# One word instead of 512 cleared between two scatters of a routed transformer kernel, with the order of work laid out anew

## The chip, the core and the metric

The kernel runs on one core of one Trainium2 chip. The time is device microseconds of one execution; where several runs are shown, the median is given with its lowest and highest. The core's engines are named as the profile names them: PE multiplies matrices (PEld is its weight load), DVE and ACT work on vectors, POOL (GpSimd) does small vector work and issues the scatters, SP (SyncE) issues the plain transfers. Each engine runs its own instructions strictly in the order in which the program emitted them; between engines semaphores hold an instruction until what it reads is there.

## What is computed

Two layers over `x` of 4 batches x 512 tokens x 128 features, each layer a cross-attention (16 heads of 8, against a context of 77 positions) and then a mixture of 8 experts of which each token uses 2:

```python
x = x + tanh(g_xattn[0]) * L0_xattn(layernorm(x), ctx_1024, Wq, Wk, Wv, Wo, bo)
x = x + tanh(g_ffn[0])   * L0_ffn(layernorm(x), w_router, w1, b1, w2, b2)
x = x + tanh(g_xattn[1]) * L1_xattn(layernorm(x), ctx_1024, ..., positions, mask)
x = x + tanh(g_ffn[1])   * L1_ffn(layernorm(x), gate_w, w1, b1, w2, b2)
```

In L0_ffn and L1_ffn a softmax over 8 router logits gives two experts and their weights; each expert is 128 -> 512 -> GELU -> 128 with biases, and the two results are added with their weights. In the second layer's attention a position bias and a mask are added to the scores, and the softmax has 1 added to its denominator.

## The kernel before

All arithmetic is in f32. A batch of 512 tokens is held as 128 partitions x 4 tokens. The four batches form two groups of two, and each group of 1024 tokens is routed by itself, in each layer: every token is written twice (once for each of its two experts) to a DRAM table `xg` in which each expert has a region of rows. The tokens are then read back in blocks of rows that belong to one expert, 7 blocks of 256 rows and 9 of 128 for each group, multiplied with that expert's weights, and the result rows are written to a second DRAM table `yk`, at rows that belong to the tokens. Last the two result rows of each token are loaded and added to `x`.

Both writes are scatters: POOL issues an indirect DMA that writes 128 rows, one from each partition, to the rows named by 128 indices. There are 64 into `xg` (4 batches x 4 x 2 for each of two layers) and 92 into `yk` (one for each 128 rows of a block). `Scatters.send` issues them all. Ahead of each it clears 512 words on one partition of `fill`, the tile of zeros that was written to the `xg` tables at the start. No scatter reads that tile.

What is emitted when is written out by hand in the text `ORDER`; an engine meets its instructions in that order. A word is a layer, a part, a number, and a batch or group after the dot:

- Attention of a batch: `LS` statistics, `LT` shift and norm, `LU` transposition, `Q` queries, `S0` to `S3` scores and their maxima (DVE, line 297), `M` minus the maximum, `W0`, `W1` that put into the queries, `X0` to `X3` scores once more and exponentials (ACT, line 335), `U0` to `U3` product with the values (PE, line 343), `E`, `T`, `N` division, `F` output projection and residual.
- Routing of a batch: `RS`, `RT`, `RU` the norm again, `RL` logits, `RC`, `RD` the two experts, `RM`, `RN` places by counting, `RX` the row numbers, `Z0` to `Z3` the scatters into `xg`, two in each.
- For a group: `RB` the table of blocks, `RG` its transposition and the read of the blocks' first rows into registers of SP (line 572). Everything that SP issues after this read in the order waits behind it.
- A block of a group: `w` load of the expert's weights (line 599, five buffers), `x` load of its rows (line 607, six buffers), `t` transposition, `u` first product and GELU (lines 634 and 640), `d` second product, bias and weight (lines 649 to 668), `y` its one or two scatters into `yk` (eight buffers).
- `CL`, `CA`: load of a batch's result rows and addition to `x`.
- At the start: `fill` clears the tile of zeros (DVE), `clear00` to `clear11` write it to the four `xg` tables (SP, lines 744 and 750), `vclear` clears a tile for values (POOL), `second` prepares constants of the second layer (POOL, from the loads of positions), `mask`, `routing`, `gate` prepare theirs.

The scatters of one target are declared independent of each other, so one does not wait for another's data; each eighth one waits for the scatter eight earlier, whose semaphore it uses again.

Of the kernel before, what the change touches and what calls it, by code (L numbers as in the profile page):

```python
# [8 lines left out]
F32 = mybir.dt.float32  # L9
# [7 lines left out]
B, S, D = 4, 512, 128  # L17
# [25 lines left out]
def flamingo_kernel(ctx: ExitStack, tc: tile.TileContext, a: dict, out: bass.AP):  # L43
    nc = tc.nc
# [3 lines left out]
    const = ctx.enter_context(tc.tile_pool(name="const", bufs=1))  # L48
# [51 lines left out]

    ident = const.tile([P, P], F32, tag="ident", name="ident")
    make_identity(nc, ident)
    mhalf = const.tile([P, NT], F32, tag="mhalf", name="mhalf")
    nc.gpsimd.memset(mhalf, -0.5)

# [280 lines left out]
    class Scatters:  # L386
# [4 lines left out]

        def send(self, to, rows, index):

            nc.gpsimd.memset(fill[:1, 0, :S], 0.0)  # L394
            i = nc.gpsimd.indirect_dma_start(  # L395
                out=to[:, :], out_offset=bass.IndirectOffsetOnAxis(ap=index, axis=0), in_=rows, in_offset=None
            )
            for other in self.sent:
                tc.declare_no_dep(i.ins, other.ins, reason="each pair has a row of its own")
            self.sent.append(i)  # L400
# [334 lines left out]
    fill = const.tile([P, 2, CAP // P * PAY], F32, tag="fill", name="fill")  # L735
# [75 lines left out]
    def part(l, name, n):  # L811
# [18 lines left out]
            }[name]()  # L830

    ORDER = """
        vclear3 vclear0 fill vclear2 0LS.0 keys0 gate values0 0LT.0 0LS.2 0LU.0 0LS.1 0LS.3 0Q.0 0LT.1 0LT.2 values3
        0S1.0 0S0.0 0S2.0 0LU.1 0LU.2 0S3.0 0Q.1 clear10 0M.0 vclear1 mask0 0W0.0 0LT.3 0S0.1 0W1.0 0S3.1 clear00
        0X0.0 0S1.1 0Q.2 values1 mask1 0S2.2 mask2 0X1.0 0S2.1 0U0.0 0M.1 0X2.0 routing 0U1.0 0X3.0 0E0.0 0W0.1 0U2.0
        0X0.1 0T0.0 0U3.0 0X1.1 0W1.1 0U0.1 0E1.0 0S1.2 0U1.1 0T1.0 clear01 mask3 0S0.2 0E0.1 0LU.3 clear11 0N.0 0T0.1
        0X2.1 0F.0 0RS.0 0X3.1 values2 0U2.1 0RT.0 0S3.2 0U3.1 0M.2 0E1.1 second 0Q.3 0W0.2 0RU.0 0T1.1 0W1.2 0S2.3
        0N.1 0RL.0 0RC.0 0F.1 0RS.1 0X0.2 0X1.2 0RD.0 0U0.2 0X2.2 0RM.0 0RN.0 0RX.0 0U1.2 0Z0.0 0RT.1 0S1.3 0U2.2
        0RU.1 0Z1.0 0S3.3 0RL.1 0S0.3 0X3.2 0RC.1 0M.3 0RD.1 0Z2.0 0U3.2 0W0.3 0RM.1 0E0.2 0T0.2 0X0.3 0RN.1 0RX.1
        0RB.1 0E1.2 0Z3.0 0X1.3 0Z0.1 0T1.2 0N.2 0RG.1 0U0.3 0W1.3 0w0.0 0Z1.1 0F.2 0Z2.1 0Z3.1 0x0.0 0U1.3 0RS.2  # L840
        0E0.3 0X2.3 0x1.0 0X3.3 0RT.2 0w1.0 0U2.3 0U3.3 0E1.3 0T0.3 0RU.2 0T1.3 0RL.2 0N.3 0RC.2 0t0.0 0x2.0 0t1.0
        0F.3 0RD.2 0x3.0 0w2.0 0x4.0 0u0.0 0u1.0 0RS.3 0RM.2 0d0.0 0x5.0 0w3.0 0w4.0 0w5.0 0y0.0 0RT.3 0d1.0 0t2.0
        0t3.0 0RN.2 0x6.0 0u2.0 0RU.3 0RX.2 0t4.0 0w6.0 0u3.0 0x7.0 0Z0.2 0d2.0 0u4.0 0t5.0 0RL.3 0t6.0 0d3.0 0x8.0
        0RC.3 0u5.0 0Z1.2 0RD.3 0RM.3 0d4.0 0u6.0 0RN.3 0y1.0 0d5.0 0d6.0 0RX.3 0w7.0 0w8.0 0Z2.2 0t7.0 0u7.0 0RB.3
        0w9.0 0x9.0 0y2.0 0d7.0 0w10.0 0Z3.2 0t8.0 0Z0.3 0RG.3 0t9.0 0w0.1 0x10.0 0w11.0 0u8.0 0Z1.3 0d8.0 0x11.0
        0Z2.3 0u9.0 0Z3.3 0t10.0 0w12.0 0d9.0 0x12.0 0u10.0 0y3.0 0x13.0 0d10.0 0w13.0 0x0.1 0t11.0 0t12.0 keys1 0x1.1
        0u11.0 0w1.1 0u12.0 0d11.0 0t0.1 0y4.0 0w14.0 0t1.1 0y5.0 0d12.0 0x2.1 0x14.0 0u0.1 0t13.0 0w2.1 0u1.1 0d0.1
        0y6.0 0x15.0 0y7.0 0u13.0 0y8.0 0y9.0 0y10.0 0x3.1 0t14.0 0t2.1 0w15.0 0d1.1 0u2.1 0w3.1 0t3.1 0y11.0 0d13.0
        0u14.0 0t15.0 0d2.1 0w4.1 0u15.0 0x4.1 0x5.1 0w5.1 0d14.0 0x6.1 0y12.0 0w6.1 0y13.0 0y14.0 0x7.1 0d15.0 0u3.1
        0t4.1 0t5.1 0x8.1 0w7.1 0d3.1 0u4.1 0t6.1 0u5.1 0y15.0 0d4.1 0t7.1 0u6.1 0x9.1 0CL.0 0t8.1 0w8.1 0y0.1 0y1.1  # L850
        0CA.0 1LS.0 0CL.1 0d5.1 0u7.1 0x10.1 0w9.1 0CA.1 1LT.0 0x11.1 0d6.1 0t9.1 0u8.1 0t10.1 0d7.1 1LU.0 1LS.1 0u9.1
        0d8.1 0y2.1 0y3.1 1Q.0 0t11.1 0w10.1 1LT.1 0x12.1 1S0.0 0w11.1 0d9.1 0y4.1 0y5.1 1S1.0 0x13.1 1LU.1 0u10.1
        0t12.1 0w12.1 1S2.0 0y6.1 0x14.1 0d10.1 0u11.1 0x15.1 1Q.1 0t13.1 0y7.1 1S3.0 0u12.1 0d11.1 0t14.1 0w13.1
        1S2.1 0y8.1 0w14.1 1S0.1 0d12.1 1M.0 0y9.1 0u13.1 0w15.1 1S3.1 1W1.0 0y10.1 0u14.1 0d13.1 1W0.0 0y11.1 0t15.1
        1S1.1 0y12.1 0u15.1 1X0.0 0d14.1 0d15.1 0y13.1 0y14.1 1X1.0 0y15.1 1U0.0 1M.1 1X2.0 1U1.0 0CL.2 1W0.1 1E0.0
        0CL.3 1X3.0 0CA.2 1U2.0 1X0.1 1LS.2 1U3.0 1E1.0 1T0.0 1X1.1 1W1.1 1LT.2 1T1.0 1U0.1 1N.0 1X2.1 1U1.1 1LU.2
        1F.0 0CA.3 1RS.0 1E0.1 1X3.1 1T0.1 1Q.2 1LS.3 1RT.0 1S1.2 1S3.2 1RU.0 1S2.2 1LT.3 1U2.1 1S0.2 1M.2 1U3.1 1E1.1
        1RL.0 1T1.1 1W0.2 1LU.3 1RC.0 1RD.0 1N.1 1X0.2 1F.1 1X1.2 1RS.1 1Q.3 1RM.0 1RN.0 1RX.0 1Z0.0 1W1.2 1RT.1 1S0.3
        1S1.3 1U0.2 1RU.1 1Z1.0 1S2.3 1RL.1 1X2.2 1U1.2 1Z2.0 1RC.1 1RD.1 1RM.1 1X3.2 1Z3.0 1RN.1 1RX.1 1S3.3 1Z0.1
        1M.3 1U2.2 1U3.2 1E0.2 1T0.2 1Z1.1 1E1.2 1Z2.1 1W0.3 1T1.2 1X0.3 1W1.3 1RB.1 1Z3.1 1N.2 1X1.3 1F.2 1U0.3 1RG.1  # L860
        1x0.0 1RS.2 1X2.3 1RT.2 1w0.0 1U1.3 1E0.3 1RU.2 1X3.3 1RL.2 1t0.0 1U2.3 1w1.0 1x1.0 1RC.2 1U3.3 1E1.3 1u0.0
        1RD.2 1RM.2 1RN.2 1x2.0 1RX.2 1x3.0 1x4.0 1T0.3 1T1.3 1N.3 1Z0.2 1F.3 1x5.0 1Z1.2 1t1.0 1w2.0 1RS.3 1d0.0
        1u1.0 1y0.0 1RT.3 1d1.0 1RU.3 1t2.0 1t3.0 1RL.3 1RC.3 1w3.0 1w4.0 1u2.0 1u3.0 1RD.3 1RM.3 1t4.0 1Z2.2 1RN.3
        1RX.3 1RB.3 1d2.0 1x6.0 1t5.0 1Z3.2 1Z0.3 1u4.0 1d3.0 1w5.0 1w6.0 1w7.0 1w8.0 1RG.3 1t6.0 1u5.0 1Z1.3 1x7.0
        1d4.0 1x8.0 1u6.0 1t7.0 1x9.0 1w9.0 1Z2.3 1Z3.3 1d5.0 1x10.0 1d6.0 1u7.0 1d7.0 1y1.0 1t8.0 1x11.0 1x0.1 1y2.0
        1w0.1 1u8.0 1y3.0 1t9.0 1y4.0 1u9.0 1t10.0 1t0.1 1x1.1 1d8.0 1w10.0 1u0.1 1d9.0 1t1.1 1u10.0 1t11.0 1y5.0
        1y6.0 1x2.1 1w11.0 1d0.1 1u11.0 1d10.0 1w1.1 1w2.1 1x3.1 1u1.1 1x4.1 1t2.1 1w3.1 1w4.1 1t3.1 1d1.1 1x5.1
        1w12.0 1y0.1 1y1.1 1u2.1 1y7.0 1d11.0 1x12.0 1w5.1 1x13.0 1u3.1 1t4.1 1d2.1 1t12.0 1u4.1 1d3.1 1w6.1 1u12.0
        1w13.0 1y8.0 1d4.1 1w7.1 1d12.0 1t5.1 1t13.0 1u5.1 1x6.1 1u13.0 1y2.1 1d5.1 1d13.0 1x14.0 1w14.0 1y9.0 1t14.0
        1y3.1 1w15.0 1u14.0 1d14.0 1y4.1 1t6.1 1u6.1 1x15.0 1y10.0 1x7.1 1x8.1 1x9.1 1t15.0 1w8.1 1y11.0 1t7.1 1y12.0  # L870
        1y5.1 1y13.0 1d6.1 1u7.1 1d7.1 1t8.1 1w9.1 1u15.0 1u8.1 1x10.1 1x11.1 1y6.1 1t9.1 1d8.1 1x12.1 1u9.1 1t10.1
        1y7.1 1y8.1 1w10.1 1d15.0 1d9.1 1u10.1 1t11.1 1t12.1 1d10.1 1w11.1 1x13.1 1u11.1 1w12.1 1d11.1 1u12.1 1y14.0
        1x14.1 1w13.1 1w14.1 1y15.0 1w15.1 1t13.1 1d12.1 1t14.1 1y9.1 1y10.1 1x15.1 1y11.1 1y12.1 1u13.1 1d13.1 1u14.1
        1CL.0 1t15.1 1u15.1 1d14.1 1y13.1 1y14.1 1CL.1 1d15.1 1y15.1 1CA.0 1CA.1 1CL.2 1CL.3 1CA.2 1CA.3
    """
    for word in ORDER.split():
        if "." in word:
            name, n = word.split(".")
# [74 lines left out]
```

## Time and profile before

| what | us |
|---|---|
| median of 3 runs (lowest to highest) | 453.98 (452.78 to 454.99) |
| the profiled execution, its own time | 449.32 |
| its span, from first to last instruction | 447.6 |
| PE busy, granted clock over the span | 394.7, 0.97 |
| POOL busy | 296.0 |
| of it: 156 scatters / 156 clears | 152.1 / 80.3 |
| of it: 16 roots (line 210), 8 additions (line 694) | 17.0, 10.2 |
| DVE / ACT busy | 243.9 / 225.0 |
| DMA: 81.19 MB, mean GB/s | 181 |

The profile is one execution. "Busy" is the time in which an engine had an instruction at work; a group of instructions is given by line, engine, operation and tile, with its count, busy time and mean nanoseconds of one, and then the idle time of the engine just before them with what ended it. The times of the scatters into `xg`, from the timeline: layer 0, first group 81.1 to 107.8, second group 126.4 to 158.8; layer 1, first group 285.2 to 311.7, second group 328.6 to 360.9. The last matmul ends at 433.6; the last scatter's rows land at 438.0, then the results are loaded, added and stored.

### The profile page before, as it was taken

How to read it: one execution, taken by the hardware profiler on the slowest of the kernel's cores; microseconds unless marked ns; L12 is line 12 of the kernel's file. 1: busy time of each engine (PE TensorE's matmuls, PEld its weight loads, DVE VectorE, ACT ScalarE, POOL GpSimd, SP SyncE). 2: the span in 40 equal slices, each digit the busy share in tenths (PEclk: the TensorE clock that was granted, in tenths of full speed). 3: DMA queues.
4: the chain of work that ended last, by engine and by line, in shares of the span. 5: the costliest groups of instructions: out<-in, count | busy, mean ns of one | idle time of the engine just before them, and what ended most of it. 6: DMA issues, size and time to landing. Idle time of an engine off the chain costs nothing.

```text
span 447.6 us, 9040 instructions
## 1 busy us (share of the span) xinstructions
PE 394.7 (88%) x2936; PEld 279.9 (63%) x2936; DVE 243.9 (54%) x929; ACT 225.0 (50%) x529; POOL 296.0 (66%) x480
## 2 busy tenths in 40 slices
PE   2399999979999599999999999999889989998960
PEld 1166345534988489996774355544378878987960
DVE  7777478763746443437682367776256533332442
ACT  3256756646564345356437764544538434433540
POOL 3478312787298889867885430698159988888870
PEclk9999999999999989999999999999689999999995
DMA  7999940014756497976613000011914568777855
GB/s 196 331 401 400 401 161 2 24 43 113 265 182 198 132 296 241 305 274 191 207 42 113 7 1 2 17 39 42 308 55 148 163 208 300 263 250 230 304 205 193
DMA packets 38526, 81.19 MB, mean 181 GB/s; under 512 B 6236, under 2 KB 20316, under 8 KB 38480
## 3 DMA queue, kind: packets, MB, share of 16 engines
q1 hardware_dynamic: 32336, 69.51, 46.6%
q0 software_dynamic: 4992, 10.30, 6.5%
q10 hardware_dynamic: 1152, 0.82, 0.7%
q8 instruction: 23, 0.38, 0.3%
q14 instruction: 23, 0.19, 0.1%
HBM read 51.69 MB, written 28.91 MB: 180 GB/s over the span
## 4 chain that ended last, share of the span: by engine, by line
PE 31%; POOL 7%; DVE 5%; DMA 4%; issue 4%; ACT 1%; SPq 0%; POOLq 0%; DVEq 0%; ACTq 0%
PE mm L649 8%; PE mm L634 7%; POOL xg L395 3%; PE mm L329 3%; DMA xb<-xg 2%; POOL fill L394 2%; PE o L343 2%; PE mm L289 2%; PE mm L326 2%; PE mm L279 1%; PE mm L266 1%; POOL yk L395 1%; PE mm L382 1%; DMA y<-yk 1%; PE mm L619 1%
## 5 line engine op out<-in xcount | busy, mean ns | idle before, releaser
L640 ACT ACTIVATE h<-mm,w 128x128 f32<-128x128 f32 (+1 forms) x256 | 86.7, 414 | 105.4 <-issue 82.6
L395 POOL DMA_INDIRECT yk<-yb,to x92 | 89.6, 974 | 20.6 <-issue 12.7
L634 PE MATMUL mm<-xbT,w 128*128 128x128 f32 (+1 forms) x512 | 92.4, 325 | 8.5 <-DVE xbT L621 6.9
L649 PE MATMUL mm<-w,h 128*128 128x128 f32 x736 | 96.6, 283 | 0.8 <-ACT h L640 0.2
L649 PEld LDWEIGHTS mm<-w,h 128*128 128x128 f32 x736 | 90.7, 194 | 5.2 <-ACT h L640 2.9
L634 PEld LDWEIGHTS mm<-xbT,w 128*128 128x128 f32 x512 | 76.2, 193 | 17.1 <-DVE xbT L621 9.1
L335 ACT ACTIVATE eT<-mm 77x512 f32<-77x512 f32 x128 | 65.3, 592 | 32.7 <-PE mm L329 32.6
L394 POOL MEMSET fill<- 1x512 f32 x156 | 80.3, 515 | 0.1
L395 POOL DMA_INDIRECT xg<-rows,rows_to x64 | 62.5, 976 | 24.2 <-issue 21.3
L657 DVE TENSOR_TENSOR yb<-mm,w 128x256 f32<-128x256 f32 (+1 forms) x64 | 22.3, 349 | 73.8 <-PE mm L649 70.9
L297 DVE TENSOR_REDUCE mx<-mm 128x4 f32<-128x308 f32 x128 | 52.1, 471 | 15.7 <-PE mm L289 15.6
L209 POOL TENSOR_SCALAR rstd<-mv 128x4 f32<-128x4 f32 x16 | 3.7, 230 | 75.1 <-DVE mv L207 35.0
L329 PE MATMUL mm<-qa,kb 32*77 32x512 f32 x256 | 43.6, 632 | 0.3 <-DVE qa L317 0.3
L343 PE MATMUL o<-eT,vb 128*32 128x512 f32 x256 | 37.5, 635 | 0.0
L621 DVE COPY xbT<-mm 128x256 f32<-128x256 f32 (+1 forms) x64 | 21.1, 344 | 25.3 <-PE mm L619 25.1
L289 PE MATMUL mm<-kb,q 32*128 32x154 f32 x512 | 30.8, 320 | 0.1
L289 PEld LDWEIGHTS mm<-kb,q 32*128 32x128 f32 x512 | 22.4, 183 | 11.7 <-issue 8.2
L663 DVE TENSOR_TENSOR yb<-yb,xb 128x256 f32<-128x256 f32 (+1 forms) x64 | 23.3, 364 | 2.2
L619 PE MATMUL mm<-ident,xb 128*128 128x128 f32 x92 | 20.0, 285 | 3.6 <-DMA xb<-xg 3.6
L329 PEld LDWEIGHTS mm<-qa,kb 32*77 32x77 f32 x256 | 11.5, 143 | 18.1 <-issue 8.7
L317 DVE TENSOR_TENSOR qa<-mm,q 128x512 f32<-128x512 f32 x16 | 11.0, 687 | 17.3 <-PE mm L315 8.9
L220 ACT ACTIVATE xn<-x,nmr,rstd 128x128 f32<-128x128 f32 x32 | 13.0, 483 | 13.2 <-DVE nmr L215 13.2
(156 smaller groups left out, 475.5 us busy)
## 6 DMA issues: line engine op xcount, KB each, us to landing
w<-in_experts SPq DMA_DIRECT2D x64, 578.0 KB, 5.1
xg<-fill SPq DMA_DIRECT2D x16, 1040.0 KB, 16.2
y<-yk SPq DMA_DIRECT2D x16, 256.0 KB, 3.2
xb<-xg SPq DMA_DIRECT2D x28, 130.0 KB, 3.8
xb<-xg SPq DMA_DIRECT2D x36, 65.0 KB, 3.9
yk<-yb,to POOLq DMA_INDIRECT x92
x<-in_x SPq DMA_DIRECT2D x4, 256.0 KB, 3.5
xg<-rows,rows_to POOLq DMA_INDIRECT x64
```

The source lines that it names most:

```text
L289: nc.tensor.matmul(view[g][:, h], lhsT=self.q[h][rows, t * P : (t + 1) * P], rhs=kbs[l][rows, h, :, b, :], start=(l == 0), stop=(l == 0 or ...
L297: nc.vector.tensor_reduce(self.mx[:, t, :, 2 * g : 2 * g + 2], view[g], AX.X, ALU.max)
L329: nc.tensor.matmul(ps[g][:KV, :], lhsT=kbs[l][rows, h, w, b, :], rhs=self.qa[h][rows, :], start=(l == 0), stop=True,)
L335: nc.scalar.activation(self.eT[j][g][:KV, :], ps[g][:KV, :], AF.Exp)
L343: nc.tensor.matmul(self.o[a][g * 32 : (g + 1) * 32, :], lhsT=vbs[self.b][:, self.l, g, j, :], rhs=self.eT[j][g], start=(w == 0), stop=(w = ...
L394: nc.gpsimd.memset(fill[:1, 0, :S], 0.0)
L395: i = nc.gpsimd.indirect_dma_start(out=to[:, :], out_offset=bass.IndirectOffsetOnAxis(ap=index, axis=0), in_=rows, in_offset=None)
L619: nc.tensor.transpose(ps[:, s * P : (s + 1) * P], x[:, s, :D], ident)
L634: nc.tensor.matmul(ps[:, g * 256 : g * 256 + n], lhsT=w[:, c * P : (c + 1) * P], rhs=xT[:, :n], start=True, stop=True,)
L640: nc.scalar.activation(h[:, c, :n], ps[:, g * 256 : g * 256 + n], AF.Gelu_apprx_tanh, bias=w[:, B1_AT + c : B1_AT + c + 1])
L649: nc.tensor.matmul(y[:, s * P : (s + 1) * P], lhsT=h[:, c, s * P : (s + 1) * P], rhs=w[:, W2_AT + c * P : W2_AT + (c + 1) * P], start=(c = ...
L663: nc.vector.tensor_tensor(yb[:, :n, :], yb[:, :n, :], x[:, :n, D : D + 1].to_broadcast([P, n, D]), ALU.mult)
```

## The change

The clear between two scatters writes one word of a tile of its own, `apart`, instead of 512 words of `fill`. Since `fill` is then read only by the transfers that clear the tables, no scatter's clear has an order against these any more; the first scatter into a table waits for the transfers that cleared it.

`ORDER` has the same words in a new sequence. All parts, their instructions and shapes are as before; what differs is when each is emitted. The two lines of code and the places in the order that the prediction speaks of:

```diff
+    apart = const.tile([1, 1], F32, tag="apart", name="apart")
...
         def send(self, to, rows, index):
-            nc.gpsimd.memset(fill[:1, 0, :S], 0.0)
+            nc.gpsimd.memset(apart, 0.0)
             i = nc.gpsimd.indirect_dma_start(
...
-        vclear3 vclear0 fill vclear2 0LS.0 keys0 gate values0 0LT.0 0LS.2 0LU.0 0LS.1 0LS.3 0Q.0 0LT.1 0LT.2 values3
+        vclear1 keys0 vclear0 0LS.0 gate second 0LT.0 fill vclear2 vclear3 clear10 0LS.1 0LU.0 0LS.2 0Q.0 0LS.3 0LT.1
...
-        0N.1 0RL.0 0RC.0 0F.1 0RS.1 0X0.2 0X1.2 0RD.0 0U0.2 0X2.2 0RM.0 0RN.0 0RX.0 0U1.2 0Z0.0 0RT.1 0S1.3 0U2.2
+        0X0.2 0W1.2 0RC.0 0N.1 0S2.3 0RD.0 0U0.2 0X1.2 0F.1 0RS.1 mask3 0X2.2 0S3.3 0RT.1 0U1.2 0RM.0 0S0.3 0RN.0
+        0RU.1 0U2.2 0RX.0 0M.3 0Z0.0 0RL.1 0RC.1 0W0.3 0E0.2 0RD.1 0X3.2 0Z1.0 0RM.1 0X0.3 0U3.2 0RN.1 0RX.1 0E1.2
...
-        0w9.0 0x9.0 0y2.0 0d7.0 0w10.0 0Z3.2 0t8.0 0Z0.3 0RG.3 0t9.0 0w0.1 0x10.0 0w11.0 0u8.0 0Z1.3 0d8.0 0x11.0
+        0w9.0 0x10.0 0t8.0 0d5.0 0d6.0 0w10.0 0u7.0 0u8.0 0x11.0 0w11.0 0x12.0 0t9.0 0RG.3 0d7.0 0d8.0 0t10.0 0u9.0
...
-        1RX.3 1RB.3 1d2.0 1x6.0 1t5.0 1Z3.2 1Z0.3 1u4.0 1d3.0 1w5.0 1w6.0 1w7.0 1w8.0 1RG.3 1t6.0 1u5.0 1Z1.3 1x7.0
+        1Z1.3 1x12.0 1Z2.3 1w11.0 1u8.0 1RG.3 1u9.0 1d8.0 1x13.0 1t10.0 1d9.0 1Z3.3 1t11.0 1w0.1 1u10.0 1x0.1 1y2.0
...
```

## The prediction

> **What bounds the kernel now.** I read the page's busy shares first, then the POOL groups, a stretch of POOL's timeline, the busy table by stretches, and last the chain that ended last.
>
> ```profile
> PE 394.7 (88%) x2936; PEld 279.9 (63%) x2936; DVE 243.9 (54%) x929; ACT 225.0 (50%) x529; POOL 296.0 (66%) x480
> ...
> L395 POOL DMA_INDIRECT yk<-yb,to x92 | 89.6, 974 | 20.6 <-issue 12.7
> ...
> L394 POOL MEMSET fill<- 1x512 f32 x156 | 80.3, 515 | 0.1
> L395 POOL DMA_INDIRECT xg<-rows,rows_to x64 | 62.5, 976 | 24.2 <-issue 21.3
> ```
>
> PE is busy 88% of the span, POOL 66%; the 156 clears that the change shrinks are 80.3 us of POOL. The timeline shows what one scatter costs when POOL has nothing else to do:
>
> ```profile
> 305.11 0.52 POOL L394 MEMSET fill<- 1x512 f32 x1
> 305.80 0.97 POOL L395 DMA_INDIRECT xg<-rows,rows_to  x1 [0.17 <-issue]
> 306.76 0.51 POOL L394 MEMSET fill<- 1x512 f32 x1
> 307.44 0.96 POOL L395 DMA_INDIRECT xg<-rows,rows_to  x1 [0.17 <-issue]
> ```
>
> From start to start 307.44 - 305.80 = 1.64 us: scatter 0.96, clear 0.51, a gap of 0.17. POOL runs at this pace almost without a break from 121 to 194, 283 to 311 and 337 to 424. Whether that sets the end is read from PE:
>
> ```profile
> core 0: us, PE busy (x) PEld busy (x) DVE busy (x) ACT busy (x) POOL busy (x), PEclk, DMA share, GB/s
> ...
> 78.00:110.00 32.00, 29.70 (x212) 13.56 (x205) 19.28 (x85) 18.27 (x39) 26.76 (x37) 0.95 0.17 52
> ...
> 121.00:160.00 39.00, 31.98 (x225) 29.63 (x225) 18.86 (x84) 16.52 (x40) 34.43 (x49) 0.96 0.57 184
> 160.00:195.00 35.00, 34.55 (x248) 31.97 (x247) 13.93 (x49) 18.64 (x52) 30.05 (x41) 1.00 0.82 259
> ...
> 311.00:328.00 17.00, 15.24 (x81) 7.12 (x79) 6.14 (x35) 9.90 (x21) 3.16 (x6) 0.80 0.68 227
> ...
> 360.00:400.00 40.00, 36.98 (x273) 34.27 (x272) 14.13 (x51) 16.75 (x49) 35.94 (x49) 1.00 0.78 251
> ```
>
> POOL is full in 160 to 195 too, yet PE is busy 34.55 of 35.00 there: PE is the bound, and POOL's pace is worth nothing. In 121 to 160 PE stands still for 7.02 us, in 311 to 328 for 1.76 us with the granted clock at 0.80. Both stretches follow a run of scatters that move tokens to their experts, and expert blocks cannot be loaded before the run has landed. The chain says so for the second layer:
>
> ```profile
> 309.09 0.96 POOL xg L395
> 310.05 0.51 POOL fill L394
> 310.56 0.17 issue
> 310.73 2.27 DMA xg<-rows,rows_to
> ```
>
> So POOL binds in four places only, the four dispatches (two groups of tokens in each of two layers), and for a moment at the end; elsewhere it is PE.
>
> **The change, part by part.** *The clear.* It goes from 512 words on one partition to one word. The trace has no one-word clear on one partition; the nearest row is one word on each of 128 partitions, "L715 POOL MEMSET region<- 128x1", 96 ns. With the gap kept, a scatter's period becomes 0.96 + 0.10 + 0.17 = 1.23 us, 0.42 less (more precisely 0.515 - 0.096); 156 x 0.42 = 65 us off POOL. Bounds for the period: below, the short clears start 0.03 to 0.04 us apart in the timeline (42.95, 42.99, 43.02), so 0.96 + 0.03 = 0.99; above, 1.64, if something that the clear covers (the rest of the preceding scatter) needs that time anyway. A loss from scatters being too close I exclude at this point: the transfer lands 2.27 us after the scatter's start, so today's 1.64 already overlaps one transfer with the next. Only if each scatter took as long as the slowest in the trace (81.11, 1.25 us) would the period be 1.25 + 0.10 + 0.17 = 1.52. I take 1.23, by the row of the same operation.
>
> The Trainium skill, "Perfetto Trace Analysis", sections "GPSIMD Engine Instruction" and "DMA Instruction — SWDGE (GPSIMD)", speaks against this: the eight cores of the engine are not synchronised, a scatter's descriptors come from the first two alone, and spans there should be judged by start-to-start spacing. A clear of one partition then keeps one core busy while the other may already be making descriptors, and the saving could be nothing; by that rule the scatters' spacing stays 1.64, and the sum is that of the third case below without its gains. The spacing of today is in the rows above; how it divides no row here shows.
>
> *The first scatter's wait.* Before, the first clear waited for all transfers that read the tile of zeros; now the first scatter waits for the clears of its own DRAM table. The last of these transfers is issued at 47.65 and ends its issue at 49.3; with 16.8 us to land that is 66 us. The first scatter runs at 81.1. Cost nothing, cover 15 us; all of POOL's queue is behind it if that cover goes.
>
> *The start.* The memset of the zeros tile (DVE, 12.03, 1.79 us, with 0.38 idle ahead of it) moves from ahead of the first batch's statistics to behind its shift: up to 2.1 us earlier for PE's first transposition at 17.61. Against it, second_layer's casts and constants (0.19 + 0.43 + 0.52 + 0.28 = 1.4 us of POOL) and two clears of value tiles (1.27 each) now stand ahead of the reciprocal roots of batches 1 to 3, which ran at 20.02; the casts also wait for the positions' loads, issued at 8.53. The clears of DRAM start some 2.8 us later, inside the cover named. I book -1 us.
>
> *First dispatch, layer 0.* Sixteen scatters end 16 x 0.42 = 6.7 us sooner. But the order now puts three scores parts, two other PE parts and their maxima of batch 3 ahead of the first scatter: on PE 3 x 0.74 + 1.0 + 0.45 = 3.7 us, over a busy share of 29.70/32 that is 4.0. Net 6.7 - 4.0, -3 us (2.7, rounded).
>
> *Second dispatch, layer 0.* 22 scatters stand between the last of the first dispatch and the last of the second: 22 x 0.42 = 9.2 us of POOL. More than PE's 7.02 us of idle time cannot be had. The order also helps: SyncE reads the block table into registers (line 572) ahead of every load queued behind it; in the trace PE waits 1.80 us at 150.62 for that table and 2.42 us at 157.21 for a load behind it. The read now comes after the load of block 12 instead of block 9, and 8.0 us more of expert matmuls stand ahead of the last scatter. I book the 4.2 us of these two waits, -4.
>
> *First dispatch, layer 1.* Again -6.7, but four scores parts (4 x 1.29), a product with values twice and three small parts come ahead of the first scatter: 8.1 us of PE, over 0.97 busy 8.4. The dispatch ends 1.7 us later against the stream of matmuls; since 1.6 us more of matmuls stand ahead of the first block now, +1 us at most is left.
>
> *Second dispatch, layer 1.* PE idles 3.17 us in 328 to 360 and 3.02 in 360 to 400, 6.2 together, part of it behind the same register read (353.69) and the load after it (354.62, 3.74 us). That read moves behind block 12 as well. Two thirds, -4.
>
> *The end.* The last scatters already wait for DVE (1.96 us at 433.72), so POOL is not behind there; two periods, 2 x 0.42, -1.
>
> Sum: -1 - 3 - 4 + 1 - 4 - 1 = -12. The profiled execution took 449.32 us (span 447.6), so 437.3; the median of the runs shown is 453.98, 4.7 above it, and the same subtraction gives 442.0. The other ends: if every idle microsecond in the four places comes back (7.0 + 2.3 in 78 to 110 + 5.2 for 311 to 328, of which 3.4 by the clock, + 6.2) and the start gives 2.1, -23, 431.
>
> **The rivals.** *Hidden by PE.* The period falls to 1.23, but the matmuls, their exponentials and the DVE work between bind everywhere: 160 to 195 speaks for it, the 7.02 us of idle PE against it. The start's -1 alone: 453.
>
> *Late dispatch.* The period stays near 1.64 (the rule above, or whatever the long clear covers), and the order, laid out for short scatters, starts its dispatches later: +4.0 and +8.4, less 1 at the start and 4.2 by the register read: +7, 461. It decides from the period at which 32 scatters of the two first dispatches no longer pay 12.4 - 5.2 = 7.2 us: 0.22 us saved each, so above 1.42. For it: nothing in the trace shows a scatter without 0.5 us of POOL work ahead. Against it: after waits of 0.63 us (418.29) and 1.96 us (433.72) the scatter still takes 0.96, so a longer distance does not change it.
>
> *A queue that stands still.* The period falls, but SyncE's later register read leaves the second group's weights and tokens so late that PE runs out of first-group blocks. Their loads take 5.1 and 3.8 us to land (medians of the page's DMA list), 8.9 us of idle PE in each layer instead of the -4: -12 + 8 + 17.8 = +14, 468. It decides once less than the load time of matmuls is left behind the read; 7.1 to 8.0 us of them were moved ahead of the last scatters, which speaks for it, and the expert weights fetched ahead (five buffers) speak against.
>
> **How the numbers follow.** Forecast 0.64, hidden 0.13, late dispatch 0.17, a standing queue 0.06. Predicted: 442. What lies within 0.5% (2.3 us) is no change that a measurement can tell. Faster: 0.64 and 0.03 of the hidden case, 0.67. Same: 0.07 of the hidden case. Slower: the last two and the other 0.03, 0.26. The range goes from 431, all idle time back, less 1 for a shorter gap, 430, to 457, which leaves out the late dispatch and the standing queue. The forecast's own range is 431 to 450.
>
> **What would show it.** Right: L395 scatters 1.2 to 1.3 us apart, still 0.96 long; a clear of about 0.1; dispatches of some 21 us instead of 27; PE idle in the stretch of the second dispatch of layer 0 under 4 us. Wrong: a spacing of 1.5 or more, or scatters longer than 1.1; first dispatches starting over 6 us later and PE idle behind them; PE busy 34 of 35 everywhere with the same span. The forecast falls first if the period does not shrink.

## The result: 512 us, slower by 13%, and the profile after

The changed kernel takes 512.39 us (median of 4 runs, 509.25 to 513.55), the kernel before 453.38 beside it: ratio 1.1291, 95% interval 1.1221 to 1.1362. The forecast was 442, the range 430 to 457. The profiled execution took 513.55 us, its span is 511.8, 64.2 longer than before's.

The page of the changed kernel, first the busy line, then POOL's groups (lines are one later than before):

```profile
PE 410.4 (80%) x2936; PEld 291.3 (57%) x2936; DVE 244.5 (48%) x929; ACT 229.4 (45%) x531; POOL 228.9 (45%) x480
...
L396 POOL DMA_INDIRECT yk<-yb,to x92 | 89.3, 971 | 115.6 <-DVE to L669 76.7
...
L396 POOL DMA_INDIRECT xg<-rows,rows_to x64 | 62.5, 977 | 23.9 <-issue 13.0
```

POOL did what was forecast: 228.9 us busy instead of 296.0, scatters still 0.97, a clear of 89 ns, and 1.27 us from one scatter's start to the next. It now waits for others: ahead of the scatters into `yk` it is idle for 115.6 us, 76.7 of them until DVE is done. PE does the same 2,936 products in 410.4 us instead of 394.7, and its idle time goes from 52.9 to 101.4. So of the 64.2 us, 48.5 are idle time of PE and 15.7 slower products. The busy table by stretches shows where:

```profile
core 0: us, PE busy (x) PEld busy (x) DVE busy (x) ACT busy (x) POOL busy (x), PEclk, DMA share, GB/s
87.00:109.00 22.00, 9.32 (x68) 4.11 (x68) 5.88 (x30) 7.64 (x15) 17.11 (x33) 0.77 0.15 49
109.00:120.00 11.00, 8.59 (x39) 4.04 (x39) 6.52 (x29) 3.10 (x6) 0.53 (x2) 0.53 0.00 0
...
158.00:190.00 32.00, 18.85 (x111) 17.72 (x112) 9.29 (x44) 7.53 (x22) 19.48 (x37) 0.73 0.54 166
190.00:225.00 35.00, 34.73 (x256) 32.71 (x256) 16.72 (x56) 18.89 (x53) 12.58 (x21) 1.00 0.83 262
400.00:425.00 25.00, 12.04 (x66) 11.03 (x67) 6.37 (x30) 6.22 (x17) 17.00 (x32) 0.69 0.38 122
```

In the stretches in which POOL sends one scatter after another (87 to 109, 158 to 190, 400 to 425) PE is idle for 41 to 58% of the time, DVE and ACT for more. Where most scatters come singly (190 to 225), PE is busy 34.73 of 35. And the granted clock falls in the stretches in which PE stands still: up to the last product it is 0.5 for 92 us in all, against 17 before. That is where the slower products come from: one of line 650 takes 280 ns at the full clock, as before, and 432 at half of it.

What do the engines wait for? The timeline of the end of the first dispatch (start, duration, engine, line; in brackets the idle time before and what ended it):

```profile
95.78 0.66 PE L316 MATMUL mm<-ident,m_pad 128*128 128x128 f32 x4
...
96.45 1.99 ACT L336 ACTIVATE eT<-mm 77x512 f32<-77x512 f32 x3 [2.40 <-remote]
...
97.10 0.66 PE L358 MATMUL mm<-ident,oT 128*128 128x128 f32 x4 [0.66 <-issue]
...
100.69 0.36 DVE L363 RECIPROCAL rden<-mm 128x32 f32<-128x32 f32 x1 [5.04 <-remote]
...
106.05 0.96 POOL L396 DMA_INDIRECT xg<-rows,rows_to  x1 [0.23 <-issue]
107.02 0.09 POOL L395 MEMSET apart<- 1x1 f32 x1
107.32 0.96 POOL L396 DMA_INDIRECT xg<-rows,rows_to  x1 [0.21 <-issue]
109.29 0.69 DVE L318 TENSOR_TENSOR qa<-mm,q 128x512 f32<-128x512 f32 x1 [7.78 <-remote]
110.13 1.15 PE L330 MATMUL mm<-qa,kb 32*77 32x512 f32 x4 [12.37 <-DVE qa L318]
```

Line 318 adds to what line 316 has put into a bank, and that was done at 96.44. Yet DVE starts at 109.29, and PE, which needs `qa` next, stands still for 12.37 us. "remote" is what the profile writes when it finds nobody who could have released the instruction at that time. The chain that ended last, asked for the same stretch, has the same holes:

```profile
95.66 5.02 another core or an unknown queue
100.67 0.02 issue
100.69 0.36 DVE rden L363
...
101.51 7.75 another core or an unknown queue
109.27 0.02 issue
109.29 0.70 DVE qa L318
```

The trace also records every rise of a semaphore. In the kernel before, all 48 signalling products that start in 85 to 112 us have such a record within 0.1 us of their end. Here PE's semaphore rises at 96.37, 97.08, 97.82, 99.23, 100.67 and 109.27, though PE's last product ended at 97.76 and its next one starts at 110.13. The rises at 100.67 and 109.27 can only belong to products done at least 2.9 and 11.5 us before, and DVE starts 23 ns after each of the two. So TensorE's signals come late, in steps of about 0.72 us or twice that (0.71, 0.74, 1.41, 1.44 in the list above; the 8.60 up to the last is twelve of them); of PE's intervals after 80 us, 30 lie in 0.70 to 0.75 or 1.40 to 1.46, against 5 before. Over the whole execution 89 rises of PE's semaphore have no signalling product that ended within 0.2 us of them; in the kernel before there is none up to the last product. The rises of DVE's, ACT's and POOL's semaphores that are on record all follow within 0.03 us of an instruction's end, in both kernels: only TensorE's are late. Later, PE itself issues slowly without waiting for anybody:

```profile
166.57 2.72 PE L650 MATMUL mm<-w,h 128*128 128x128 f32 x11 [4.09 <-issue]
171.68 0.37 PE L650 MATMUL mm<-w,h 128*128 128x128 f32 x1 [2.39 <-issue]
173.10 0.37 PE L635 MATMUL mm<-xbT,w 128*128 128x128 f32 x1 [1.05 <-issue]
174.49 1.88 PE L635 MATMUL mm<-xbT,w 128*128 128x128 f32 x8 [1.01 <-issue]
175.38 0.63 ACT L641 ACTIVATE h<-mm,w 128x128 f32<-128x128 f32 x2 [8.50 <-issue]
```

In such stretches a share of the records is missing altogether: each transfer should leave 16 records of its landing, and a scatter of the first dispatch has 0 to 9 of them here, 3 or 4 as a rule; over the execution 3,088 are left of 5,616 (before: 5,532). The rises themselves took place, since all waits were met, so a missing record by itself costs nothing; the experiments show both signs, and they do not always go together. The scatters' data is not late: the first packet of a scatter starts about 1.54 us after the scatter and the last ends at about 1.89 us (before: 1.90), in both kernels alike (medians of the first dispatch).

### The profile page after: what moved, and what is told of

Same layout as the page of the kernel before. It is cut to its first block, busy times and chain, and to the rows that moved or that the text cites. A ratio compares the mean times of both kernels' runs of the same rounds, so it can differ in the third digit from the quotient of the medians.

```text
span 511.8 us, 9040 instructions
## 1 busy us (share of the span) xinstructions
PE 410.4 (80%) x2936; PEld 291.3 (57%) x2936; DVE 244.5 (48%) x929; ACT 229.4 (45%) x531; POOL 228.9 (45%) x480
## 4 chain that ended last, share of the span: by engine, by line
PE 62%; issue 11%; DVE 9%; another core or an unknown queue 8%; ACT 5%; POOL 3%; DMA 3%; SPq 0%; DVEq 0%; POOLq 0%; ACTq 0%
PE mm L650 15%; PE mm L635 14%; PE mm L330 6%; PE o L344 5%; PE mm L290 5%; PE mm L267 3%; PE mm L620 2%; PE mm L327 2%; ACT eT L336 2%; PE mm L280 2%; PE mm L383 2%; PE mm L229 2%; DVE mx L298 1%; POOL xg L396 1%
## 5 line engine op out<-in xcount | busy, mean ns | idle before, releaser
L396 POOL DMA_INDIRECT yk<-yb,to x92 | 89.3, 971 | 115.6 <-DVE to L669 76.7
L650 PE MATMUL mm<-w,h 128*128 128x128 f32 x736 | 103.4, 292 | 27.9 <-issue 24.0
L650 PEld LDWEIGHTS mm<-w,h 128*128 128x128 f32 x736 | 96.0, 205 | 32.4 <-issue 25.8
L635 PE MATMUL mm<-xbT,w 128*128 128x128 f32 (+1 forms) x512 | 96.3, 337 | 7.1 <-issue 6.3
L635 PEld LDWEIGHTS mm<-xbT,w 128*128 128x128 f32 x512 | 80.4, 204 | 15.1 <-issue 9.1
L658 DVE TENSOR_TENSOR yb<-mm,w 128x128 f32<-128x128 f32 (+1 forms) x64 | 22.3, 348 | 77.2 <-PE mm L650 30.9
L622 DVE COPY xbT<-mm 128x128 f32<-128x128 f32 (+1 forms) x64 | 21.8, 345 | 48.6 <-remote 18.4
L620 PE MATMUL mm<-ident,xb 128*128 128x128 f32 x92 | 20.7, 285 | 10.0 <-issue 5.6
L363 DVE RECIPROCAL rden<-mm 128x32 f32<-128x32 f32 x16 | 5.7, 354 | 40.1 <-PE mm L358 21.2
L664 DVE TENSOR_TENSOR yb<-yb,xb 128x128 f32<-128x128 f32 (+1 forms) x64 | 23.3, 365 | 2.2
L327 PE MATMUL mm<-mbT,ident 77*77 77x512 bf16 x64 | 19.7, 416 | 2.0 <-issue 1.4
L620 PEld LDWEIGHTS mm<-ident,xb 128*128 128x128 f32 x92 | 12.6, 149 | 13.3 <-issue 6.9
```

The costliest lines, as they stand in the source:

```text
L327: nc.tensor.matmul(ps[g][:KV, :], lhsT=ident16[:KV, :KV], rhs=mskT[b], start=True, stop=False)
L396: i = nc.gpsimd.indirect_dma_start(out=to[:, :], out_offset=bass.IndirectOffsetOnAxis(ap=index, axis=0), in_=rows, in_offset=None)
L620: nc.tensor.transpose(ps[:, s * P : (s + 1) * P], x[:, s, :D], ident)
L635: nc.tensor.matmul(ps[:, g * 256 : g * 256 + n], lhsT=w[:, c * P : (c + 1) * P], rhs=xT[:, :n], start=True, stop=True,)
L650: nc.tensor.matmul(y[:, s * P : (s + 1) * P], lhsT=h[:, c, s * P : (s + 1) * P], rhs=w[:, W2_AT + c * P : W2_AT + (c + 1) * P], start=(c = ...
L664: nc.vector.tensor_tensor(yb[:, :n, :], yb[:, :n, :], x[:, :n, D : D + 1].to_broadcast([P, n, D]), ALU.mult)
```

## The experiments

All times are medians where no range is given; "before" beside them lay between 450.2 and 453.4 in every comparison of more than one run. The kernels with the commonest distance of two scatters as measured, the number of landing records, and the number of late signals of TensorE, counted as above (rises without a signalling product that ended within 0.2 us):

| order | cleared between two scatters | distance, us | time, us | landing records | late signals |
|---|---|---|---|---|---|
| old | 512 words (before) | 1.64 | 450 to 453 | 5,532 | 0 |
| old | 384 | 1.54 | 451.6 | 5,543 | 0 |
| old | 256 (two chips) | 1.43 | 501.5, 489.1 to 506.1 | 3,187, 3,199 | 100, 103 |
| old | 1 | 1.26 | 536.4 | 3,166 | 93 |
| old | 768 | 1.86 | 476.0 | 5,554 | 0 |
| old | 15 times 1 | 3.26 | 716.1 | 5,586 | 0 |
| new | 512 (two chips) | 1.64 | 460.0, 458.8 | 4,318, 4,374 | 4, 0 |
| new | 384 | 1.54 | 445.1 | 5,544 | 0 |
| new | 3 times 1 | 1.50 | 465.6 | 3,381 | 75 |
| new | 256 | 1.43 | 486.6 | 3,213 | 120 |
| new | 1 (after, two chips) | 1.27 | 512.4, 510.0 | 3,088, 3,067 | 89, 100 |

Every kernel of the table with a distance of 1.50 us or less has 75 or more late signals, every other one 0 to 4.

**Clear and order, each alone.** Four kernels: before's order with the one-word clear, and after's order with 512 words; then both orders with 256.

```diff
 # old_order_1: before's ORDER
-            nc.gpsimd.memset(fill[:1, 0, :S], 0.0)
+            nc.gpsimd.memset(apart, 0.0)
 # new_order_512, new_order_256, old_order_256: one line of after or before
+            nc.gpsimd.memset(fill[:1, 0, :S], 0.0)     # or :256
```

> The order of before with the one-word clear. Theory 'crowding': scatters that follow one another with only 0.3 us between them hold back the issue of instructions on all other engines, whatever the order: 490 to 525 us, with PE, ACT and DVE standing still for causes that the profile does not show while a run of scatters lasts. Rival 'order': the new order alone costs the 59 us and short clears are harmless: 430 to 452 us, period of a scatter 1.26 us, PE busy in the same places as before.

> The order of after with the clear of 512 words. Crowding: the 59 us go away with the long clear, 440 to 462 us (the prediction's case of late dispatch gave 461 for just this). Order: 500 to 515 us.

> The order of after with a clear of 256 words; the period of a scatter should be 0.96 + 0.30 + 0.17 = 1.43 us. Crowding: if the harm grows steadily as the distance shrinks, halfway between 512 words and one word, 475 to 485 us; if it sets in at a distance, either within 10 us of the run with 512 words or within 10 us of 512 us. Order: 500 to 515 us.

> The order of before with a clear of 256 words, period 1.43 us. Crowding: as for the new order, halfway (470 to 485) if the harm is steady, within 10 us of 454 or of the run with one word if it sets in at a distance. Order: 438 to 454 us, no harm, POOL's relief alone.

Ratios to before: 1.183 [1.173, 1.194], 1.018 [1.012, 1.024], 1.077 [1.071, 1.084], 1.112 [1.103, 1.122]. The short clear does the harm, and it does more of it in the old order (+86 us) than in the new one; the order softens it. The 536 lies above the 490 to 525 that were expected. With 256 words, half of the way, a good half of the harm is there already (50.6 of 85.6 us in the old order).

**How far apart is far enough.** Before's order with 384 and 768 words, and with fifteen clears of one word (`for _ in range(15)`).

> The order of before with a clear of 384 words, period 0.96 + 0.41 + 0.17 = 1.54 us. Steady harm (1.64: 451, 1.43: 501): 470 to 482 us. A threshold below 1.54: 445 to 455.

> The order of before with a clear of 768 words, period 0.96 + 0.73 + 0.17 = 1.86 us. If scatters 1.64 us apart still hold back the other engines, more distance pays: 430 to 448 us. If the harm ends at or before 1.64 us, POOL's longer runs cost (16 x 0.22 = 3.5 us in each of four dispatches): 455 to 470 us.

> The order of before, with fifteen clears of one word between two scatters: 0.09 + 14 x 0.033 = 0.55 us of POOL, about the time of one clear of 512 words. If time between scatters is what counts: 446 to 460 us. If the 512 words written are (or the one long instruction): near the run with one word, 510 to 540 us.

384 words: 1.007 [1.003, 1.012], so no harm, but no gain either. 768: 1.056 [1.048, 1.064]; no record is missing, POOL is simply the bound for longer. The fifteen clears missed their aim: each waits for the one before, which adds 0.143 us and not the few hundredths expected, so the distance became 3.26 us, for a third of the scatters 3.6 or more, and POOL the bound of everything (ratio 1.585). For the old order the limit of the harm lies between 1.54 and 1.43 us.

**Scatters beside plain streams.** A kernel of its own: products, clears on DVE and ACT copies without any wait, beside runs of twenty scatters with 512, 1, 256, 0, 384, 128, 768 words between, and other kinds of transfer.

> Not the kernel: it copies x to its output and computes nothing of the reference. PE, DVE and ACT each issue one stream of like instructions that wait for no other engine (PE's wait for nothing at all), beside runs of 20 transfers issued by POOL, with pauses of some 7 us between runs: scatters of 128 rows 512, 1, 256, 0, 384, 128, 768 words apart, then 15 one-word clears apart, scatters of 64 rows one word apart, plain POOL transfers one word apart, scatters 1024 words apart, and clears alone. Crowding: PE's rate of matmuls falls during the runs whose scatters start less than some 1.5 us apart and not at 512 words and beyond; with nothing between, most of all. If what is held back is a wait for semaphores, PE's stream keeps its rate and only streams that wait suffer. Order (or data dependence in the kernel): no stream changes its rate in any run.

Nothing slows: 8.9 to 9.0 products, 3.9 DVE and 2.9 ACT instructions per us in every run, at distances down to 1.27 us (0.57 for plain transfers). Two rows of its busy table (columns as above), the first with 512 words, the second with one:

```profile
10.00:42.00 32.00, 32.00 (x289) 32.00 (x288) 20.43 (x125) 29.02 (x95) 28.80 (x40) 1.00 0.13 43
50.00:72.00 22.00, 22.00 (x200) 22.00 (x199) 14.07 (x86) 19.97 (x65) 18.05 (x36) 1.00 0.16 53
```

So dense scatters alone hold nobody up. The next two kernels add what was missing: signals between engines (four rings PE to ACT to DVE to PE), and loads on SP's queue with DVE operands in SBUF.

> Leaves out the whole computation (the output is a copy of x). Four independent rings run beside phases of twenty scatters: TensorE multiplies into a PSUM bank, ScalarE copies the bank to SBUF, VectorE copies that to the operand of the next product of its ring, each step waiting for the other engine's signal (three signals per turn). Between the scatters of the phases GpSimd clears 512, 1, 384, 256 words, then nothing; then come plain GpSimd transfers, scatters of 64 rows, scatters of rows of 2 words (same 128 rows, 1/65 of the bytes), 512 words again, and clears alone. Theory A (signals between engines are held up while scatters follow each other closely; in the trace of after ScalarE's exponentials start 21 ns after an update of TensorE's semaphore that came 2 us after the product had ended): the turns of a ring per microsecond are the same in the pauses and with 512 and 384 words, and fall to less than half with 256 words, 1 word and nothing, and a part of the update records is missing there. With rows of 2 words the same if the 128 descriptors count, no fall if the bytes count. Rival B (the port that VectorE and GpSimd share, or the engines' own instruction supply): no fall in any phase of this kernel, as in the run before without signals. Rival C (a backlog of the scatters' queue): the landing of a scatter grows from one scatter to the next in the dense phases, above 2.4 us; the rings don't fall.

> Leaves out the whole computation (the output is a copy of x). The same phases of scatters beside streams without signals between engines: products, ScalarE copies, VectorE additions with two operands in SBUF (instead of clears that read nothing), and 360 loads of 256 KB on SyncE's queue into eight buffers in turn. Theory A (signals between engines): all three compute streams keep their rate in every phase. Rival B (port): VectorE's rate falls by over 10% in the phases with 256 words, 1 word and nothing against 512 words. Rival C (queues): the loads per microsecond fall by over 20% in these phases, or their landings stretch from one load to the next, while the compute streams keep their rates.

For rows of full length theory A failed here: the rings turn as fast beside one word as beside 512. Rows of the rings' table, in turn with 512 words, a pause (POOL clears 128 x 2048 words), with 1 and with 256:

```profile
10.00:41.00 31.00, 30.10 (x186) 24.61 (x186) 22.27 (x93) 22.32 (x93) 27.79 (x39) 1.00 0.13 42
42.00:49.00 7.00, 3.43 (x12) 2.55 (x12) 7.00 (x8) 1.59 (x6) 6.83 (x4) 0.63 0.04 12
50.00:74.00 24.00, 22.63 (x151) 19.84 (x149) 16.91 (x73) 17.63 (x74) 20.36 (x39) 0.91 0.16 54
121.00:149.00 28.00, 28.00 (x186) 26.35 (x184) 21.06 (x91) 22.88 (x92) 24.79 (x39) 0.91 0.14 47
```

186 products in 31 us are 6.0 per us, 151 in 24 are 6.3, 186 in 28 are 6.6. In the kernel with loads DVE's additions stay at 3.0 to 3.1 per us and the loads go on as well beside full rows, so neither the port (for these operations) nor a backlog of the queues does it.

The runs of scatters with rows of 2 words, 1.26 to 1.30 us apart, went otherwise. In the rings they left 0.85 of their landing records, the twenty scatters after them 0.92, and between 268 and 282 us seven signals of TensorE came up to 2.2 us late; the four runs of full rows with 1, 256, 384 and no words between had all of their records and not one late signal. In the kernel with loads these runs lie in 249 to 285:

```profile
216.00:242.00 26.00, 26.00 (x236) 26.00 (x235) 23.31 (x80) 23.59 (x77) 21.66 (x42) 1.00 1.04 385
249.00:263.00 14.00, 14.00 (x128) 14.00 (x127) 12.54 (x44) 12.70 (x41) 11.63 (x23) 1.00 1.03 235
263.00:285.00 22.00, 22.00 (x200) 22.00 (x199) 19.72 (x68) 19.97 (x65) 10.89 (x20) 1.00 1.03 122
```

The loads fall from 385 GB/s to 235 and 122, and POOL waits up to 3.58 us for a scatter's landing; the streams that wait for nobody keep their rates. So a small form of the disturbance does appear outside the whole kernel, and it isn't the bytes that bring it.

**The new order with 384 words.**

> The order of after with a clear of 384 words, so a scatter every 1.54 us. If the harm were set by the distance alone with its limit between 1.54 and 1.43 us (the old order stood at 452 with 384 and 501 with 256): 460 (the new order with 512 words) or up to 6 us less, 454 to 461. If it is set by the load of all signals together (the new order with 512 words already has 4,318 landing records of the 5,532 of before, so it is hurt in places where the old order isn't): above 464, between the 460 with 512 words and the 487 with 256.

445.12 us against 450.43: ratio 0.990 [0.986, 0.994], faster than both kernels. All landing records are there. This kernel shows what the new order does undisturbed, in two stretches that the prediction had for before:

```profile
121.00:160.00 39.00, 38.74 (x265) 35.93 (x265) 24.77 (x113) 21.19 (x50) 27.27 (x42) 0.94 0.59 188
160.00:195.00 35.00, 30.34 (x205) 27.57 (x205) 12.69 (x44) 15.79 (x46) 28.43 (x41) 0.95 0.78 257
```

PE idles 0.26 us in the first, where it idled 7.02; in the second it idles 4.66, where it idled 0.45. And it idles more around the first dispatch, which now begins at 87.6 instead of 81.1: 3.91 and 5.01 us in the first two rows below, where before had 2.30 in 78 to 110 and, in the third row, 0.53:

```profile
78.00:110.00 32.00, 28.09 (x199) 12.33 (x195) 20.72 (x90) 18.65 (x38) 25.48 (x36) 0.89 0.16 48
110.00:121.00 11.00, 5.99 (x25) 4.98 (x26) 1.73 (x5) 3.29 (x7) 3.79 (x7) 0.60 0.62 185
...
110.00:121.00 11.00, 10.47 (x70) 9.06 (x70) 7.84 (x36) 7.57 (x16) 1.96 (x4) 1.00 0.90 290
```

**Chip or distance, and the kind of clear.** 512 words being worse than 384 in the new order could have been the chip, as they ran on different ones. So these were measured together on another chip, with three clears of one word as the fourth:

> The changed kernel once more, beside the three below on one chip. The kernels with scatters at 1.27 and 1.43 us and the new order with 512 words were measured on other chips than those with 384 words. If the distance of the scatters does the harm: 505 to 515, and again fewer than 0.4 of the scatters' 16 landing records each. If it was a property of the chips that they ran on: 435 to 450, with all landing records.

> The order of after with the 512 words of before, once more. The first time it gave 460, though 384 words gave 445 on another chip; a scatter every 1.64 us instead of 1.54 can't explain more than 16 us. If it was the chip: 446 to 452 here, and nearly all landing records (0.7 of them before). If it is this distance with this order: 457 to 463 again.

> The order of before with 256 words (a scatter every 1.43 us), once more. If the distance does the harm: 495 to 505, as the first time. If the chip: 440 to 452.

> The order of after with three clears of one word between two scatters: by the 0.143 us that each of fifteen clears added (period 3.26 us against 1.27 with one), a scatter every 1.55 us, as with 384 words in one clear. If the distance alone counts: 443 to 450, as with 384 words (445). If a long clear protects the others by itself: above 480.

509.95 (ratio 1.129 [1.117, 1.140]), 458.80 (1.011 [1.001, 1.021]), 489.06 to 506.09, and 465.57 (1.031 [1.020, 1.043]). It isn't the chip. The three clears came out at 1.50 us, not 1.55, in the dispatches, and at 1.96 for 32 scatters of the combine; their time lies between the 445 of 1.54 us and the 487 of 1.43, with 75 late signals. So the distance counts and not the length of one clear, though the two theories' numbers were not clearly met. The new order with 512 words is another matter: over a fifth of its landing records is missing, but its signals are on time (4 late ones, by 0.4 to 0.8 us, and none on the second chip). Its 14 to 15 us over 384 words are within the 16 that 156 scatters, each 0.10 us later, can cost POOL. So there it isn't shown that the disturbance costs anything, and missing records alone are no proof of harm.

**The destinations.** In the kernels of streams and rings the rows went to memory in a line. So the changed kernel, with row numbers in a line too:

```diff
+            n, at = len(self.sent), inline if to.shape[1] == PAY else inline_y
...
-                out=to[:, :], out_offset=bass.IndirectOffsetOnAxis(ap=index, axis=0), in_=rows, in_offset=None
+                out=to[:, :], out_offset=bass.IndirectOffsetOnAxis(ap=at[:, n : n + 1], axis=0), in_=rows,
+                in_offset=None,
```

> The changed kernel with other destinations: the sixteen scatters of each dispatch write 128 rows in a line each (row 128n+p), and so do the combine's, instead of the rows that the routing says; so the experts compute other tokens' rows, all else is as in after (same instructions, same bytes, a scatter every 1.27 us). In the two kernels of streams and rings the destinations lay in a line as well, and nothing stood still there. Theory D (what holds the other engines up is that the rows of a scatter lie far apart in memory): 430 to 450, and 16 landing records for nearly every scatter. Theory A (the distance of the scatters and the engines' signals, wherever the rows go): 500 to 515, and 2 to 5 landing records for each scatter in the dense runs, as in after.

509.27 us, ratio 1.127 [1.116, 1.137], with 3,131 landing records and 81 late signals: as in after. Where the rows go doesn't matter.

**The shapes of PE's work**, by another kernel of its own:

> Leaves out the whole computation (the output is a copy of x). Three sets of work in turn, each beside sixteen scatters with 512 words cleared between two, then sixteen with 1 word, then sixteen with 256, with 8 us of one-partition clears before each: first TensorE's transposes of [128, 512] with VectorE's additions out of PSUM (as in lowered), then four products of 32 rows by 512 columns side by side with ScalarE's exponentials (as in exps), then products of 128 by 512 with ScalarE's copies. These are the shapes that the earlier kernels of streams and rings lacked. Theory A' (TensorE's signals come late when scatters follow each other closely and its products are of these shapes): in at least one set the rate of VectorE or ScalarE falls by over 30% in the phases with 1 word and 256 words against the phase with 512. Rival E (something that only the whole kernel has, such as its many stand-alone waits): the rates of every set are the same within 5% in all three phases, and nearly all landing records are there.

Rival E came true: the rates of each set are the same beside all three distances, and every landing record is there. Rows with 512 words, then with 1, for the transposes with DVE's additions (first two) and the products side by side with exponentials:

```profile
10.00:35.00 25.00, 22.82 (x140) 14.56 (x140) 24.03 (x35) 0.00 (x0) 22.46 (x32) 1.00 0.12 41
42.00:62.00 20.00, 18.19 (x113) 11.55 (x112) 19.20 (x29) 0.00 (x0) 16.54 (x33) 1.00 0.15 51
...
130.00:154.00 24.00, 24.00 (x74) 11.84 (x72) 0.00 (x0) 18.42 (x38) 21.46 (x31) 0.50 0.13 43
162.00:182.00 20.00, 20.00 (x63) 9.87 (x60) 0.00 (x0) 15.04 (x31) 16.64 (x32) 0.50 0.15 50
```

**Half of the rows in a dispatch.** Last, the changed kernel with 64 rows in each scatter of the dispatch, so that half of the rows never reach the experts, and the combine's scatters with row numbers in a line, as in `after_inline`:

```diff
+            n = len(self.sent)
+            if to.shape[1] == PAY:
+                rows, index = rows[: P // 2], index[: P // 2]
+            else:
+                index = inline_y[:, n : n + 1]
             nc.gpsimd.memset(apart, 0.0)
```

> The changed kernel with dispatches of half the size: each scatter of the dispatch sends 64 rows instead of 128, so the second half of every tile's rows never reaches the experts; the combine's scatters keep 128 rows (in a line each, which changed nothing in the run before). A scatter of 64 rows came every 1.20 us in the kernel of streams, so the distance is as in after and the rows per microsecond are 53 instead of 101 (and 83 with 384 words, where nothing stands still). Read in the first dispatch of layer 0 (88 to 108 us in after). If the rows per microsecond do the harm: there at least 14 of 16 landing records for each scatter, and TensorE's signals on time. If the number of scatters per microsecond does it: 2 to 6 of 16, and signals up to 12 us late, as in after. The time itself is mixed: 500 to 512 if the distance decides, 470 to 495 if the rows do, as the combine's scatters stay dense.

422.41 us (2 runs), ratio 0.937 [0.925, 0.949]: below every number expected. The stretch that showed the hole in after:

```profile
95.83 0.66 PE L317 MATMUL mm<-ident,m_pad 128*128 128x128 f32 x4
...
96.30 0.89 POOL L402 DMA_INDIRECT xg<-rows,rows_to  x1 [0.23 <-issue]
...
96.53 0.69 DVE L319 TENSOR_TENSOR qa<-mm,q 128x512 f32<-128x512 f32 x1 [0.77 <-PE mm L317]
...
97.50 0.89 POOL L402 DMA_INDIRECT xg<-rows,rows_to  x1 [0.22 <-issue]
```

The same addition now starts 0.04 us after the transposes have ended (95.83 + 0.66 = 96.49), with scatters 1.20 us apart. All 16 landing records are there for each scatter of this dispatch, none of PE's, DVE's, ACT's and POOL's signals is late or missing in 80 to 112, and no signal of TensorE is late in the whole execution. What was not expected is the rest. The combine's scatters still have 128 rows and still come every 1.27 to 1.28 us, and they hurt nobody either:

```profile
core 0: us, PE busy (x) PEld busy (x) DVE busy (x) ACT busy (x) POOL busy (x), PEclk, DMA share, GB/s
87.00:109.00 22.00, 18.70 (x123) 7.48 (x123) 12.64 (x60) 12.93 (x27) 17.26 (x36) 0.92 0.20 52
...
152.00:168.00 16.00, 15.40 (x111) 13.98 (x111) 7.44 (x26) 9.77 (x28) 13.13 (x25) 1.00 0.92 306
200.00:219.00 19.00, 19.00 (x203) 14.93 (x202) 14.35 (x46) 7.70 (x24) 15.61 (x30) 1.00 0.52 163
```

PE is busy 15.40 of 16 and 19.00 of 19 there, while in the kernel with whole dispatches the same kind of run (231 to 246) has 0.20 of its landing records, and PE is busy 7.54 of 15 us. So neither scatters nor rows per microsecond is the rule by itself: a dispatch of 128 rows at this distance leaves something behind that makes later scatters harmful, or the halved data matters in a way not seen.

**What is shown and what stays open.** Shown: the harm comes with the short clear, on each of the chips on which it was tried; it goes with late signals of TensorE, which come at 1.50 us and below and not from 1.54 on; in the dispatch POOL and the scatters' data are on time. In this kernel the dispatch's scatters of 128 rows are needed for it, even for the harm in the combine (one experiment); scattered destinations are not. Open: why TensorE's signals are late, where the 0.72 us come from, what is carried from a dispatch to a later combine, why 512 words in the new order lose records, and why the kernels of streams, rings and products stay undisturbed beside full rows. One rival was not tested at all: the timed runs were recorded like the profiled ones (each has its span and granted clock), so the recording may have a part in the lateness, or be the whole of it.

## Why the prediction was wrong

- *The clear and the period.* Right: 1.23 forecast, 1.27 measured, the clear 0.089 where 0.096 was taken; POOL lost 67.1 us of work where 65 was forecast. So the signs named for being right (distance, length of scatter and clear, a dispatch of some 21 us) nearly all came, with a time 70 us above the forecast: they looked at POOL alone. The reading of the Trainium skill that was weighed ("Perfetto Trace Analysis", "GPSIMD Engine Instruction" and "DMA Instruction — SWDGE (GPSIMD)") would have left the distance at 1.64; its advice to judge by start-to-start distances is what showed that it didn't stay there.
- *"A loss from scatters being too close I exclude at this point: the transfer lands 2.27 us after the scatter's start, so today's 1.64 already overlaps one transfer with the next."* This step failed. It looked only at the transfers, and these indeed do not mind. The harm falls on the other engines, whose signals from TensorE come late (89 in the changed kernel, none before), and which the sum charged nothing: with the one-word clear, 86 us in the old order; in the new order 67 us between 1.54 us of distance (445) and 1.27 (512). The bounds for the period (0.99 to 1.64) had a price on POOL alone, so no end of the range could reach the result.
- *First dispatch, layer 0.* It takes 20.7 us (87.6 to 108.3) as forecast, 6.0 less than before. But it begins 6.5 us later than before's 81.1, where 4.0 was booked; with 384 words it begins at 87.6 too, so this belongs to the order. A term mis-sized by 2.5. "First dispatches starting over 6 us later and PE idle behind them" was a sign named for being wrong, and it came, with 384 words as well: 8.9 us idle in 78 to 121 instead of 2.8.
- *Second dispatch, layer 0, and the later register read.* Right in its mechanism: with 384 words PE's 7.02 us of idle time in 121 to 160 fall to 0.26, though 4.2 of the 6.8 us come back as idle time in 160 to 195. Net 2.5, where 4 was booked, with a quarter of the cut in the clear.
- *First dispatch, layer 1.* Forecast to end 1.7 us later against the matmuls. In after it runs from 330.6 to 356.6, with the harm of what came before in it, so this term can't be read there; nor can the ends of the sum. In the second dispatch of layer 1 (328 to 400) PE idles 4.67 us with 384 words instead of 6.19: 1.5 less where 4 was booked.
- *The rivals.* "Hidden by PE" fails: the order with 384 words is faster. "Late dispatch" named 461 for a distance of 1.64, and 460.0 and 458.8 came out for just that distance, with dispatches that begin later as it said; a part of the records is missing in these runs, but with 4 and 0 late signals nothing shows that another reason was needed. Its point of decision (above 1.42 slower, below it faster) is reversed by the runs: at 1.54 the order gains 5, at 1.43 it loses 36. "A queue that stands still" fails with the idle time of 0.26.
- *The gain that was expected* isn't imaginary: with 384 words, about a quarter of the cut, 5.3 us are had, and they are had only with the new order (the old one with 384 words gives 1.007). And with dispatches of 64 rows, 1.20 us apart and undisturbed, 28 us are had, more than the 23 of the forecast's far end; that kernel sends less, so it doesn't price the same change.

## What to carry to other kernels

Before work is taken out of the space between two transfers, ask what else that space has been paying for: here 0.4 us of useless clearing per scatter was worth more than the 65 us of POOL that it cost. Change such a distance in steps and look at the other engines, not only at the one that was freed: idle time that ends with "remote" or "issue" while the supposed releaser has long been done is the sign. It is the late signals that go with lost time; missing records alone do not. Where it can be had, time both kernels without recording too, which wasn't done here. And where a change has two parts, measure each alone; the order was worth 1%, once it got a distance that it could live with.

## What the runs showed of the hardware

- With scatters of 128 rows 1.27 us apart, TensorE's signals came up to 11.5 us after its products in the stretch shown, in steps of some 0.72 us, while the scatters' data was on time; later PE also issued products without a wait, up to 4.09 us after the ones before. The signals of the other engines that are on record were never late (within 0.03 us).
- VectorE's copies from SBUF to SBUF (128 x 128, f32) take 0.24 us beside the scatters (22.27 us for 93); beside POOL's clears of 128 x 2048 words they take 0.88 by the same count (7.00 for 8) and 1.84 to 2.62 each by their own records, which overlap; VectorE's additions of two operands in SBUF keep their 3.0 to 3.2 per us beside the same clears.
- Products of 32 rows by 512 columns, four side by side and PE never idle, ran at a granted clock of 0.50 when PE had nothing else to do, with 74 products in 24 us (1.08 us each); products of 128 rows in the same kernel had 1.00. Among other products, in the kernel before, the same shape took 0.63 us.
- A POOL clear of one word costs 89 ns by itself and 0.143 us in a row of clears of the same word, since each waits for the one before.
